# Set 0's routing and placing in tiles of the context, three scatters a step, and the last layer's inverse roots on VectorE

## The chip, the cores and the metric

The kernel runs on one core of one Trainium2 chip. The metric is device time in microseconds (us) of one execution. A profiled execution gives a trace: every instruction of the engines with start and length, the waits between them, the transfers, and the clock granted to TensorE. Engines are named as in the profile: PE (TensorE, matmuls; PEld its weight loads), DVE (VectorE), ACT (ScalarE), POOL (GpSimd), SP (SyncE, which here only issues transfers).

## The reference

A decoder of two layers on x of 32 x 128 tokens by 128 features, everything in float32. Each layer adds three blocks to x, each applied to a layer norm of x without weights:

```python
x = x + L0_attn(ln(x)); x = x + L0_xattn(ln(x), ctx); x = x + L0_ffn(ln(x))
x = x + L1_attn(ln(x)); x = x + L1_xattn(ln(x), ctx); x = x + L1_ffn(ln(x))
```

L1_attn is an attention by random features (16 heads, 32 features each), L1_xattn a softmax attention over ctx (16 heads of 8). The last block, L1_ffn, is a mixture of 16 experts, 4 of them for each token, and one expert for all:

```python
logits = x @ gate_w.T
sel = top_k(logits + expert_bias, 4)
g = softmax(logits[sel])                 # weights of the four
out = swiglu(x, shared) + sum(g[e] * swiglu(x, expert e) for e in sel)
```

## The kernel before, in words

Tokens come in 8 groups (`NG`) of 4 batches (`GB`) of 128 tokens. x and ctx stay in SBUF, as `x0..x7` and `ctx0..ctx7` (`cx[g]` in the code, 128 x 512 each). For the last mixture four sets of 8 batches (`NBR`, two groups) are formed. Set 1 is computed densely: every expert on every token, with weights of zero for those not chosen (`dense_n`). Sets 0, 2 and 3 (`SETS`) are sorted by expert: each token's normalized row is written four times to a table in DRAM (`rows_in`), at places that make the rows of an expert stand together, padded to tiles of 128; then tile after tile is computed with its one expert's weights, written to `rows_out`, and gathered back.

What is done for a sorted set, in `Tables`:

- `route` (line 1997 on): VectorE, with one exponential on ScalarE, makes the four best experts of each token, a one-hot `ones` for each of the four, a `mask`, and the softmax weights `parts`. It is a generator of some 18 pieces; `choose(n, k)` in `mixture` advances it by k pieces, and `routing` runs the first piece.
- `placed` (from line 2034): 18 matmuls on PE count the tokens of each expert (`places`), VectorE turns the counts into a place for each token and choice (`place`), and into the expert that owns each tile (`of`). It has thirteen pieces. The scratch it shares with `route` comes from `two_wide` (two views of 128 x 512) and `square` (128 x 256).
- `way_out` (line 2093): indirect transfers issued by GpSimd, one for each batch and choice, which scatter 128 rows each to `rows_in`: 32 for a set.
- `way_back` (line 2201): the gathers from `rows_out`, again on GpSimd, and `added` (line 2211), which adds them to x on VectorE.

For set 0 the scratch was the tiles `rot` and `rotsin` of the pool `early`, which the first layer-1 attention uses for its rotation until step 29 or 30. For the sets of the last layer it is made in that layer's own pool.

The order of the work is written out by hand. `steps` (line 1188) takes stages as (stage, first step, every, how often). In each step the main stages run their pieces in the order of the list; after each such piece one piece is taken from the stages under `between`, in the order of that list, and what is left of `between` at the end of the step is issued there in one block. Within a region of manual order each engine issues its instructions in exactly this order, so an engine that waits holds back all that is behind it. The second layers (`second_layers`, line 2531) and the last layer (`last_layer`, line 2108) are two such regions; the order between the two on an engine is the scheduler's, as far as the data allow.

In the second layers (their steps run to 45) the stages around the change are: the averages of the cross attention, `xaverage`, one batch a step in steps 13 to 44, each with a 32 x 32 transpose (`by_token`, line 1295), a reciprocal (`rec`, 1297) and three more instructions on VectorE, and after each fourth three instructions on GpSimd (`in_range`, lines 1314 to 1316) which check the reciprocals; `totals` with its `sb` on VectorE (line 2457); `xnorm` in steps 10, 14, ... 38 and `xscaled` one step later, the norm before the cross attention, whose inverse root is GpSimd's (`power`, lines 1097 and 1098) and whose result `xn` (line 1126) PE transposes into `pxn` (line 1135). Set 0's `routing` is in step 25, `choose` in steps 26 and 27 (three pieces each) and 31 and 32 (six each), `placed` in step 33 in one go, `way_out` in steps 35 to 42 with the four scatters of one batch a step, `owned` in step 36.

In the last layer the norms of set 1 are due in step 0, of set 2 in step 1, of set 3 in step 5 (`norm`, line 2118: eight `bn_stats` and `bn_aggr` pairs on VectorE, lines 1115 and 1116, then `power` on GpSimd for each group); `chosen` of set 2 in step 5, its `placed` in step 6, its scatters from step 7; those of set 3 in steps 11, 12 and 13 on. The first tile quads of set 0 are loaded in step 0 (`rows_of`, line 2152: SP loads `rows`, then the weights of four tiles) and transposed by PE in step 1 (`prows`, line 2176). A quad goes through `rows_up` (pg, pu, then the product `sgrows` on VectorE, line 2189) and `rows_down` (`pyrows`). Twelve quads make a set, so set 2's first is needed in step 12.

Of the kernel before, what the change touches and what calls it, by code (L numbers as in the profile page):

```python
# [9 lines left out]
F32 = mybir.dt.float32  # L10
I32 = mybir.dt.int32
AF = mybir.ActivationFunctionType
ALU = mybir.AluOpType
AX = mybir.AxisListType

B, S, D = 32, 128, 128
T = B * S
GB = 4
# [4 lines left out]
E = 16  # L23
# [932 lines left out]
def fast_decoder(ctx: ExitStack, tc: tile.TileContext, ins, spans, out: bass.AP):  # L956
# [3 lines left out]
    nc = tc.nc  # L960

    res = ctx.enter_context(tc.tile_pool(name="res", bufs=1))
    st = ctx.enter_context(tc.tile_pool(name="st", bufs=4))
# [33 lines left out]
    x = [res.tile([128, GB, D], F32, name=f"x{g}") for g in range(NG)]  # L997
    cx = [res.tile([128, GT], F32, name=f"ctx{g}") for g in range(NG)]
# [82 lines left out]
    def rsqrt(dst, src):  # L1081


        n = src.shape[1]
        t = st.tile([128, n], F32, name=f"newton{n}", bufs=2)
        nc.vector.tensor_scalar(t.bitcast(I32), src.bitcast(I32), 1, None, ALU.logical_shift_right)
        nc.vector.tensor_scalar(dst.bitcast(I32), t.bitcast(I32), -1.0, float(0x5F3759DF), ALU.mult, ALU.add)
        for _ in range(3):
            nc.vector.scalar_tensor_tensor(t, dst, -0.5, dst, ALU.mult, ALU.mult)
            nc.vector.tensor_tensor(t, t, src, ALU.mult)  # L1090
            nc.vector.scalar_tensor_tensor(dst, t, 1.5, dst, ALU.add, ALU.mult)
            yield
# [16 lines left out]
    def moments(src):  # L1109

        n = src.shape[1]
        parts = st.tile([128, n, 6], F32, name=f"parts{n}")
        mv = st.tile([128, n, 2], F32, name=f"mv{n}")
        for b in range(n):
            nc.vector.bn_stats(parts[:, b, :], src[:, b, :])
            nc.vector.bn_aggr(mv[:, b, :], parts[:, b, :])  # L1116
            yield
        return mv
# [23 lines left out]
    def norm_factors(g):  # L1142
        mv = yield from moments(x[g])
        return mv, power(mv[:, :, 1], 1e-5, -0.5, "r")

    def layernorm(wk, g):
        return at_once(normed(wk, g, *at_once(norm_factors(g))))

# [543 lines left out]
    NBR = 8  # L1692
# [267 lines left out]
    class Tables:  # L1960


        def __init__(self, early, spare, C):

            self.C = C
            self.xn, self.ones, self.masks, self.parts, self.places, self.of, self.owners = ({} for _ in range(7))
            self.one = by_rows.tile([128, 1], F32, name="one")
            nc.vector.memset(self.one, 1.0)
            self.spare = spare[:, 0 : NBR * D].rearrange("p (g b f) -> p g b f", b=GB, f=D)
            self.wide = lambda: early.tile([128, GB, 2 * D], F32, name="rot", bufs=1).rearrange("p b f -> p (b f)")  # L1970
            self.thin = lambda: early.tile([128, 2, D // 2, 2], F32, name="rotsin", bufs=2).rearrange(
                "p n h d -> p (n h d)"
            )
            self.pool_of_owners = by_rows

        def later(self, wk):

            self.wide = lambda: wk.tile([128, 8 * NBR * E], F32, name="two_wide", bufs=1)
            self.thin = lambda: wk.tile([128, E * E], F32, name="thin", bufs=1)
            self.pool_of_owners = wk  # L1980

        def two_wide(self):

            t = self.wide()
            return (
                t[:, i * 4 * NBR * E : (i + 1) * 4 * NBR * E].rearrange("p (k b e) -> p k b e", k=4, e=E)
                for i in range(2)
            )

        def square(self):  # L1990
            return self.thin().rearrange("p (a b) -> p a b", b=E)
# [98 lines left out]
            self.owners[n] = self.pool_of_owners.tile([1, S], I32, name=f"owner{n}", bufs=1)  # L2090
            nc.vector.tensor_copy(self.owners[n], pt)

        def way_out(self, n, u):
            b, g = u % GB, n * NBR // GB + u // GB
            for k in range(4):
                sent = nc.gpsimd.indirect_dma_start(  # L2096
                    out=rows_in[n],
                    out_offset=bass.IndirectOffsetOnAxis(ap=self.places[n][:, k, u : u + 1], axis=0),
                    in_=self.xn[g][:, b],
                    in_offset=None,  # L2100
                )

                tc.declare_no_dep(sent.ins, group=f"rows{n}", reason="rows of different places")
                tc.add_to_no_dep_group(f"rows{n}", sent.ins)
                nc.gpsimd.nop()
                yield

    def last_layer(tag, W, stages, of_expert, tables):

        wk = phase(tag, mixture_psum)  # L2110
# [5 lines left out]
        of_set = lambda n: range(n * NBR // GB, (n + 1) * NBR // GB)  # L2116

        def norm(g):
            factors[g] = yield from norm_factors(g)

        def scaled(g):
            xn[g] = wk.tile([128, GB, D], F32, name="xr", bufs=6)
# [162 lines left out]
        def each(stage, keys):  # L2285
            return lambda k: stage(*keys[k])

        def several(stage, keys):
            def run(_):
# [5 lines left out]
        dense_n = ({1, 2, 3} - set(SETS)).pop()  # L2295
        n2, n3 = SETS[1:]
        batches = lambda n: [(n, u) for u in range(NBR)]
        once = lambda stage, k, s: (lambda _: stage(k), s, 1, 1)
        steps(
            *((lambda _, i=i: fetched(*i), at_step, 1, 1) for i, at_step in fetches),  # L2300
# [23 lines left out]
                once(chosen, n2, 5),  # L2324
                once(several(norm, of_set(n3)), None, 5),
                once(tables.placed, n2, 6),
                *((each(tables.way_out, batches(n2)[i::2]), 7, 1, 4) for i in range(2)),
                once(several(scaled, of_set(n3)), None, 8),
                once(chosen, n3, 11),
                once(tables.placed, n3, 12),  # L2330
                (each(tables.way_out, batches(n3)), 13, 1, NBR),
                (each(way_back, batches(0)), 21, 1, NBR),
                (each(added, batches(0)), 24, 1, NBR),
                (each(way_back, batches(n2)), 29, 1, NBR),
# [196 lines left out]
    def second_layers(stages, early, late, after, tables):  # L2531

        wk = phase("l1", attention_psum)
        late.append(wk)
        norm, scaled, turn_in, project, turn, features_q, features_k, totals, average, finish = stages
        xnorm, xscaled, xvalues, xkey, xturn, xproject, xweights, xaverage, xfinish = l1_xattn(early, wk)
        rnorm, rscaled, rturn, routing, choose, send, *_ = after
        R = NBR // GB
        first = lambda stage: lambda g: stage(early, g)
        later = lambda stage: lambda g: stage(g + 1)  # L2540
        norm_, scaled_ = later(norm), later(scaled)
        of_four = lambda stage, b, at: (lambda g: stage(g * GB + b), at + b, 4, NG)
        placed = lambda _: tables.placed(0)

        steps(
            (totals, 5, 1, NU),
            (later(turn), 6, 4, NG - 1),
            (finish, 9, 4, NG),
            (xfinish, 17, 4, NG),
            (xvalues, 11, 4, NG),  # L2550
            (features_k, 4, 4, NG),
            (features_q, 3, 4, NG),
            (xturn, 11, 4, NG, xscaled),
            of_four(xweights, 1, 12),
            of_four(xweights, 2, 12),
            (xaverage, 13, 1, NU),
            (later(turn_in), 4, 4, NG - 1),
            (first(rturn), 20, 4, R),
            (xkey, 11, 4, NG),
            of_four(xweights, 3, 12),  # L2560
            (average, 5, 1, NU),
            of_four(xweights, 0, 12),
            (later(project), 5, 4, NG - 1),
            (xproject, 11, 4, NG),
            (first(routing), 25, 1, 1),
            (lambda _: tables.owned(0), 36, 1, 1),
            between=[
                (xscaled, 11, 4, NG),
                (scaled_, 3, 4, NG - 1),
                (norm_, 0, 4, NG - 1),  # L2570
                (xnorm, 10, 4, NG),
                (first(rscaled), 19, 4, R, xturn),
                (first(rnorm), 18, 4, R),
                (lambda _: choose(0, 3), 26, 1, 2),
                (lambda _: choose(0, 6), 31, 1, 2),
                (placed, 33, 1, 1),
                (lambda u: tables.way_out(0, u), 35, 1, NBR),
            ],
            as_written=8,
        )  # L2580
# [41 lines left out]
    with tc.tile_pool(name="l1early", bufs=1, reuse_waits="tile") as early:  # L2622
        late = []
        W1A, W1X, L = (load(name, nc.sync, early) for name in ("w1a", "w1x", "later"))
        with scope():
            stages = []

            def l1_setup(_, k):
                stages.extend(l1_attn(early, late))

            mixture_layer(
                "l0f",
                mixture0,
                ((l1_setup, 10, 1, 1), *((lambda _, k, i=i: stages[i](k), 11 + i, 1, 1) for i in range(5))),
            )
        (W1F, load_w1f), spare = load_wide(nc.sync, "w1f")
        load_w1f()
        C = load("last", nc.sync, by_rows)
        tables = Tables(early, spare, C)
        of_expert = lambda c: (W1F["gud"][:, bass.ts(3 * c + i, 128)] for i in range(3))  # L2640
        mixture1 = mixture("l1f", W1F, lambda lg, _: tables.route(lg, 0), 1, True, of_expert, tables.kept)
        with scope():
            second_layers(stages, early, late, mixture1, tables)
# [37 lines left out]
```

## Time and profile before

| | us |
|---|---|
| three runs | 1398.26, 1410.21, 1411.42; median 1410.21 |
| the profiled execution | 1399.19 |
| its span, first to last instruction | 1397.4 |
| mean granted clock of PE in it | 0.954 of full |
| PE busy | 1251.7 |
| VectorE busy | 860.9 |
| ScalarE busy | 576.9 |
| GpSimd busy | 528.0 |

Times inside the trace are counted from the first instruction. The second layers end at about 1109 us, the last layer fills the rest. "Busy" adds up the lengths of an engine's instructions; where an engine sat idle, the profile names what ended the wait, and the step at fault is the one whose instruction came last. A clock of 0.5 in a stretch means that PE's instructions there take about twice as long.

### The profile page before, as it was taken

How to read it: one execution, taken by the hardware profiler on the slowest of the kernel's cores; microseconds unless marked ns; L12 is line 12 of the kernel's file. 1: busy time of each engine (PE TensorE's matmuls, PEld its weight loads, DVE VectorE, ACT ScalarE, POOL GpSimd, SP SyncE). 2: the span in 40 equal slices, each digit the busy share in tenths (PEclk: the TensorE clock that was granted, in tenths of full speed). 3: DMA queues.
4: the chain of work that ended last, by engine and by line, in shares of the span. 5: the costliest groups of instructions: out<-in, count | busy, mean ns of one | idle time of the engine just before them, and what ended most of it. 6: DMA issues, size and time to landing. Idle time of an engine off the chain costs nothing. (4 is left out here: it accounts for less than half of the span.)

```text
span 1397.4 us, 27515 instructions
## 1 busy us (share of the span) xinstructions
PE 1251.7 (90%) x10753; PEld 842.1 (60%) x10753; DVE 860.9 (62%) x2283; ACT 576.9 (41%) x848; POOL 528.0 (38%) x717
## 2 busy tenths in 40 slices
PE   3689999999999999699999989988987688799997
PEld 2357777777777777444444446655664386577753
DVE  5646767686767675376865535676776346534663
ACT  1354454454554433233232235555553444344432
POOL 5233232434351221132100114344425605576775
PEclk8789999999999999899999999999997879999999
DMA  9601111111212111264164120000000269699943
GB/s 346 186 1 32 32 32 32 32 33 32 51 26 47 36 32 32 64 148 91 32 122 87 36 96 2 2 2 1 2 2 26 70 189 323 201 344 305 330 142 97
DMA packets 89529, 129.07 MB, mean 92 GB/s; under 512 B 9872, under 2 KB 63760, under 8 KB 87984
## 3 DMA queue, kind: packets, MB, share of 16 engines
q1 hardware_dynamic: 76624, 102.59, 26.1%
q0 software_dynamic: 6144, 12.60, 3.1%
q10 hardware_dynamic: 6624, 12.05, 2.3%
q8 instruction: 87, 1.43, 0.5%
q14 instruction: 50, 0.41, 0.1%
HBM read 99.34 MB, written 27.85 MB: 91 GB/s over the span
## 5 line engine op out<-in xcount | busy, mean ns | idle before, releaser
L1280 ACT ACTIVATE e<-scores 128x1024 f32<-128x1024 f32 x128 | 124.0, 1021 | 58.4 <-PE scores L977 58.4
L977 PE MATMUL y<-sg,wide 128*128 128x512 f32 x224 | 117.6, 613 | 7.4 <-DVE sg L2229 2.5
L977 PE MATMUL pg<-hx,wide 128*128 128x512 f32 x224 | 116.0, 599 | 0.0
L977 PE MATMUL pu<-hx,wide 128*128 128x512 f32 x224 | 115.4, 597 | 0.0
L2204 POOL DMA_INDIRECT back<-rows_out,place x96 | 93.4, 973 | 36.4 <-issue 25.2
L1126 POOL TENSOR_SCALAR xn<-x,mv,r 128x128 f32<-128x128 f32 x76 | 63.2, 838 | 91.5 <-PE pxn L1135 82.8
L1295 DVE STREAM_TRANSPOSE by_token<-sums 128x512 f32<-128x512 f32 x64 | 45.6, 713 | 82.1 <-PE sums L977 81.8
L1531 ACT ACTIVATE e<-xscores 128x1024 f32<-128x1024 f32 x64 | 62.0, 1021 | 79.9 <-PE xscores L977 79.9
L1097 POOL TENSOR_SCALAR r<-mv 128x4 f32<-128x4 f32 x48 | 11.5, 240 | 218.7 <-DVE mv L1116 218.3
L1882 ACT ACTIVATE sg<-pg 128x512 f32<-128x512 f32 x72 | 43.0, 597 | 119.4 <-PE pg L977 108.8
L977 PE MATMUL scores<-qb,k 32*128 32x512 f32 x512 | 77.4, 675 | 12.3 <-ACT qb L1466 4.5
L1883 DVE TENSOR_TENSOR sg<-sg,pu 128x512 f32<-128x512 f32 x72 | 49.3, 685 | 61.1 <-PE pu L977 58.1
L977 PE MATMUL sums<-e,v 128*32 128x128 f32 x2048 | 73.8, 285 | 13.6 <-POOL v L1075 10.6
L1097 POOL TENSOR_SCALAR r2x<-mv 128x2 f32<-128x2 f32 x16 | 3.7, 233 | 211.7 <-DVE mv L1116 211.7
L977 PEld LDWEIGHTS sums<-e,v 128*32 128x32 f32 x2048 | 54.8, 113 | 42.2 <-issue 11.3
L2096 POOL DMA_INDIRECT rows_in<-xr,place x64 | 62.5, 976 | 34.6 <-issue 18.0
L1545 DVE COPY v<-pval 128x512 f32<-128x512 f32 x64 | 43.5, 680 | 50.3 <-PE pval L977 50.3
L1579 ACT COPY av<-po 128x512 f32<-128x512 f32 x64 | 37.5, 586 | 89.6 <-PE po L977 89.5
L977 PEld LDWEIGHTS pu<-hx,wide 128*128 128x128 f32 x224 | 42.6, 191 | 52.5 <-issue 50.1
L977 PE MATMUL po<-e,v 128*64 128x128 f32 x1024 | 65.3, 279 | 8.6 <-DVE v L1545 8.6
L977 PE MATMUL po<-av,wide 128*128 128x256 f32 x256 | 63.3, 403 | 8.6 <-DVE av L1599 8.6
L977 PEld LDWEIGHTS y<-sg,wide 128*128 128x128 f32 x224 | 35.9, 189 | 58.0 <-DVE sg L1885 36.7
(301 smaller groups left out, 2906.7 us busy)
## 6 DMA issues: line engine op xcount, KB each, us to landing
row_weights<-in_w1f_dram SPq DMA_DIRECT2D x144, 192.0 KB, 4.3
factor<-factors SPq DMA_DIRECT2D x64, 256.0 KB, 5.1
share<-combined SPq DMA_DIRECT2D x32, 512.0 KB, 10.3
rows_in<-in_few SPq DMA_DIRECT2D x36, 256.0 KB, 4.1
rows<-rows_in SPq DMA_DIRECT2D x36, 256.0 KB, 5.3
rows_out<-yrows ACTq DMA_DIRECT2D x36, 256.0 KB, 4.0
share<-combined SPq DMA_DIRECT2D x8, 1024.0 KB, 9.3
wide<-in_w1f_dram SPq DMA_DIRECT2D x1, 3272.0 KB
```

Source lines behind the costliest of these rows:

```text
L977: last[0] = nc.tensor.matmul(*args, **kw)
L1097: nc.gpsimd.tensor_scalar(t, src, add, None, ALU.add)
L1126: eng.tensor_scalar(n[:, b, :], x[g][:, b, :], mv[:, b, 0:1], r[:, b : b + 1], ALU.subtract, ALU.mult)
L1280: nc.scalar.activation(e[-1], ps[:, bass.ts(n, 2)].rearrange("p c i s -> p (c i) s"), AF.Exp, scale=scale)
L1295: nc.vector.transpose(tt.rearrange("p i t r -> p (i t r)"), po.rearrange("p i s -> p (i s)"))
L1531: nc.scalar.activation(e[-1], ps[:, n].rearrange("p r c s -> p (r c) s"), AF.Exp, scale=scale)
L1545: nc.vector.tensor_copy(v[:, bass.ts(n, XC), :], pv)
L1579: nc.scalar.copy(avs[w][n][:, :, bass.ts(b, S)], po)
L1882: nc.scalar.activation(sg, pg, AF.Silu)
L1883: nc.vector.tensor_tensor(sg, sg, pu, ALU.mult)
L2096: sent = nc.gpsimd.indirect_dma_start(out=rows_in[n], out_offset=bass.IndirectOffsetOnAxis(ap=self.places[n][:, k, u : u + 1], axis=0), in ...
L2204: nc.gpsimd.indirect_dma_start(out=outs[n, u][:, k], out_offset=None, in_=rows_out[n], in_offset=bass.IndirectOffsetOnAxis(ap=places[n][:, ...
```

## The change

Set 0's scratch is now three context tiles: `cx[0]` and `cx[1]` for the two wide views, the first 256 columns of `cx[2]` for the square. The context of a group is last read by `xvalues` and `xkey` of that group, in steps 11, 15 and 19 for these three. `two_wide` takes two tiles instead of two halves of one, in the last layer too.

With that scratch the pieces are laid out anew: `choose` advances by three pieces in each of the steps 26 to 31; the thirteen pieces of `placed` go by five in steps 32, 33 and 34 (`some_of`); `way_out` takes a list of (batch, choice) and issues three scatters in each of the steps 35 to 45, the last two of the 32 in step 45. In the last layer `way_out` gets the same four of a batch as before.

The last layer's `norm` takes its inverse roots from `norm_factors_by_vector`: one addition, and then `rsqrt`, which is the bit trick and three Newton steps, eleven instructions on VectorE, all on 128 x 4.

```diff
+    def norm_factors_by_vector(g):
+        mv = yield from moments(x[g])
+        ve = st.tile([128, GB], F32, name="ve", bufs=2)
+        nc.vector.tensor_scalar(ve, mv[:, :, 1], 1e-5, None, ALU.add)
+        r = st.tile([128, GB], F32, name="rv", bufs=2)
+        yield from rsqrt(r, ve)
+        return mv, r
...
-            self.wide = lambda: early.tile([128, GB, 2 * D], F32, name="rot", bufs=1).rearrange("p b f -> p (b f)")
-            self.thin = lambda: early.tile([128, 2, D // 2, 2], F32, name="rotsin", bufs=2).rearrange(
-                "p n h d -> p (n h d)"
-            )
+            self.wide = lambda: [cx[i] for i in (0, 1)]
+            self.thin = lambda: cx[2][:, 0 : E * E]
...
-            self.wide = lambda: wk.tile([128, 8 * NBR * E], F32, name="two_wide", bufs=1)
+            self.wide = lambda: [wk.tile([128, 4 * NBR * E], F32, name=f"wide{i}", bufs=1) for i in range(2)]
...
-        def way_out(self, n, u):
-            b, g = u % GB, n * NBR // GB + u // GB
-            for k in range(4):
+        def way_out(self, n, some):
+            for u, k in some:
+                b, g = u % GB, n * NBR // GB + u // GB
...
         def norm(g):
-            factors[g] = yield from norm_factors(g)
+            factors[g] = yield from norm_factors_by_vector(g)
...
-        placed = lambda _: tables.placed(0)
+        placing = []
+        to_send = [(u, k) for u in range(NBR) for k in range(4)]
+
+        def some_of(placing, n):
+
+            if not placing:
+                choose(0)
+                placing.append(tables.placed(0))
+            for _ in range(n):
+                if next(placing[0], "end") == "end":
+                    return
+                yield
...
-                (lambda _: choose(0, 3), 26, 1, 2),
-                (lambda _: choose(0, 6), 31, 1, 2),
-                (placed, 33, 1, 1),
-                (lambda u: tables.way_out(0, u), 35, 1, NBR),
+                (lambda _: choose(0, 3), 26, 1, 6),
+                (lambda n: some_of(placing, 5), 32, 1, 3),
+                (lambda i: tables.way_out(0, to_send[3 * i : 3 * i + 3]), 35, 1, 11),
```

The helper that the new norms call, which the kernel had for another use:

```python
    def rsqrt(dst, src):
        n = src.shape[1]
        t = st.tile([128, n], F32, name=f"newton{n}", bufs=2)
        nc.vector.tensor_scalar(t.bitcast(I32), src.bitcast(I32), 1, None, ALU.logical_shift_right)
        nc.vector.tensor_scalar(dst.bitcast(I32), t.bitcast(I32), -1.0, float(0x5F3759DF), ALU.mult, ALU.add)
        for _ in range(3):
            nc.vector.scalar_tensor_tensor(t, dst, -0.5, dst, ALU.mult, ALU.mult)
            nc.vector.tensor_tensor(t, t, src, ALU.mult)
            nc.vector.scalar_tensor_tensor(dst, t, 1.5, dst, ALU.add, ALU.mult)
            yield
```

More of the change, by code (lines that the diff above doesn't have):

```diff
@@ L1960, in fast_decoder, with __init__ @@
     class Tables:
-        def __init__(self, early, spare, C):
+        def __init__(self, spare, C):
             self.C = C
@@ L1982, in two_wide @@
         def two_wide(self):
[L1984 to L1988, printed above, removed]
+            return (t.rearrange("p (k b e) -> p k b e", k=4, e=E) for t in self.wide())
         def square(self):
@@ L2297, in last_layer @@
         batches = lambda n: [(n, u) for u in range(NBR)]
+        to_send = lambda n: [(n, [(u, k) for k in range(4)]) for u in range(NBR)]
         once = lambda stage, k, s: (lambda _: stage(k), s, 1, 1)
@@ L2326, in last_layer @@
                 once(tables.placed, n2, 6),
-                *((each(tables.way_out, batches(n2)[i::2]), 7, 1, 4) for i in range(2)),
+                *((each(tables.way_out, to_send(n2)[i::2]), 7, 1, 4) for i in range(2)),
                 once(several(scaled, of_set(n3)), None, 8),
@@ L2330, in last_layer @@
                 once(tables.placed, n3, 12),
-                (each(tables.way_out, batches(n3)), 13, 1, NBR),
+                (each(tables.way_out, to_send(n3)), 13, 1, NBR),
                 (each(way_back, batches(0)), 21, 1, NBR),
@@ L2638, in fast_decoder @@
         C = load("last", nc.sync, by_rows)
-        tables = Tables(early, spare, C)
+        tables = Tables(spare, C)
         of_expert = lambda c: (W1F["gud"][:, bass.ts(3 * c + i, 128)] for i in range(3))
```

## The prediction, on record before the run

> **What bounds the kernel now.** The page first: TensorE is busy nine tenths of the span, so time is lost only where TensorE waits, and where its clock drops after a wait.
>
> ```profile
> PE 1251.7 (90%) x10753; PEld 842.1 (60%) x10753; DVE 860.9 (62%) x2283; ACT 576.9 (41%) x848; POOL 528.0 (38%) x717
> ```
>
> Next the table by stretches around the change: the second layers' last steps (to about 1109 us) and the last layer. Columns: stretch, length, busy time (count) of PE, PE weight loads, VectorE, ScalarE, GpSimd, then the granted clock, DMA share, GB/s.
>
> ```profile
> 1030.00:1040.00 10.00, 9.03 (x111) 7.19 (x111) 6.02 (x15) 4.64 (x5) 1.86 (x6) 1.00 0.01 2
> 1040.00:1050.00 10.00, 5.89 (x72) 4.38 (x71) 9.31 (x32) 2.10 (x3) 0.00 (x0) 0.81 0.00 0
> 1050.00:1060.00 10.00, 8.17 (x54) 4.40 (x52) 4.58 (x14) 1.27 (x2) 6.01 (x7) 0.51 0.05 15
> ...
> 1110.00:1120.00 10.00, 4.82 (x19) 4.14 (x20) 0.85 (x4) 2.46 (x3) 1.49 (x4) 0.55 0.65 180
> ```
>
> VectorE is full (9.31 of 10) where PE is at its worst, then PE runs ten microseconds at half clock. The timeline of PE names the waits (start, length, instruction, in brackets the idle time before it and its releaser).
>
> ```profile
> 1046.77 1.08 PE L977 MATMUL fsums<-qphi,sb 128*32 128x128 f32 x16 [4.11 <-DVE sb L2457]
> 1080.45 1.47 PE L1135 MATMUL pxn<-in_few,xn 128*128 128x128 f32 x4 [5.59 <-DVE xn L1126]
> 1114.45 1.09 PE L2176 MATMUL prows<-in_few,rows 128*128 128x128 f32 x4 [5.42 <-DMA rows<-rows_in]
> 1212.41 1.08 PE L2176 MATMUL prows<-in_few,rows 128*128 128x128 f32 x4 [6.76 <-DMA rows<-rows_in]
> ```
>
> The first is the placing of set 0 drained at one step's end, ahead of `sb` on VectorE's queue. The third and fourth are sets 0 and 2 waiting for the last scatter. GpSimd's timeline shows how the scatters end and what their start waits for:
>
> ```profile
> 1108.08 0.96 POOL L2096 DMA_INDIRECT rows_in<-wide,place  x1 [0.30 <-DVE rec L1297]
> 1109.34 0.96 POOL L2096 DMA_INDIRECT rows_in<-wide,place  x1 [0.30 <-issue]
> 1110.38 0.56 POOL L1314 TENSOR_SCALAR in_range<-rec 128x64 f32<-128x64 f32 x1
> ...
> 1167.54 1.09 POOL L2096 DMA_INDIRECT rows_in<-xr,place  x1 [5.91 <-DVE expert_ends L2082]
> ```
>
> Set 2's 32 scatters start as soon as VectorE has placed and run without a gap to 1208.5. The chain that ended last runs back through them into VectorE's work of 1149 to 1167, set 3's eight statistics (1156.93 to 1160.0) included. From 1230 on PE and GpSimd are both full, so a shift of 1212 is a shift of the end.
>
> **The change part by part** (negative is a gain).
>
> *Placing over steps 32 to 34.* The thirteen pieces were all due in step 33; now five come in step 32, five in 33, three in 34, one per stage of PE's work. From step 32's `by_token` (1029.60) to the last statistic before the cross-attention's next group (1051.06) VectorE needs 21.5 us, 3.8 of them waits for PE (0.75, 1.57, 0.68, 0.77). The last three pieces (1044.91 to 1046.30, 1.4 us) move behind the statistics; of the waits I take half as filled, 1.9: -3.3. What is late next is that group's `xn`, after GpSimd's two-step root (0.23 and 1.04 us). With the long stall gone, 1053.04 to 1060.3 should run at full clock: pxn, sums, pk, scores then take 0.66, 1.08, 1.13, 1.14 and a 0.4 wait, 4.4 instead of 7.3: -2.9. Together -6.2. Ends: -8.7 (the whole 4.11, and 4.6 for fsums, pS, pval, sums, pk, scores, which took 1.08, 1.97, 2.02, 1.94, 2.08, 1.71 us here and 0.62, 1.10, 1.11, 1.08, 1.13, 1.14 at full clock), and -1.4. I take the middle, nearer the better end, since VectorE is the bound there.
>
> [...] The row shows 13 us at half. [...]
>
> *Routing over steps 26 to 31.* `ones`, mask, product, reductions (0.89, 0.3, 0.77, 0.68, 0.4, 0.4, 0.2 us) leave steps 31 and 32 for 28 to 31: some 3 us of VectorE work into 999 to 1020, where it is busy 7.0 and 7.7 of 10 us and PE is nearly full. Hidden by those gaps: +0.5; all of it would be +3.1 if the rotation's inputs slip. The tiles ctx0 to ctx2 were last read in step 19; nothing waits for them. The exponential moves two steps on ScalarE, which has a gap of 3.36 us at 1017 to 1020: nothing. The last layer's wide tile cut in two holds the same bytes and costs nothing. The 18 `places` matmuls (2.1 us) only change step.
>
> *Three scatters a step.* In the code step 44 first runs the last average with its three `in_range` instructions on GpSimd, and only then step 44's three scatters and step 45's two. Before, all 32 stood ahead of that check. GpSimd's queue is in order, so five scatters now wait for `rec` of the last batch (done at 1107.82 before). Then: check 1.36 (1110.38 to 1111.74), gap 0.17, four pitches of 1.264 and one of 0.96: the last scatter ends 7.6 us after `rec`, before 2.5 (1110.30). Behind it stand SyncE's first `rows` load and the four weight loads queued after that, and PE's prows. +5.1. Ends: +1.3 if only step 45's two stood behind the check, +6.5 if GpSimd is also late from earlier steps (steps of 3.3 us, 3.8 us of scatters).
>
> *Roots by VectorE.* Each group drops GpSimd's 0.23 and 1.04 us and adds twelve VectorE instructions on 128x4, each dependent on the last. No row has one in such a chain: bounds are 0.15 (L2085, 128x1, 153 ns) and 0.21 (start to start of L2061, 128x16, and its successor). I take 0.19, nearer the upper since the chain is dependent: 2.3 a group, 4.56 a set (3.6 to 5.0).
> Set 2 (step 1): the instructions follow 1125.5 and push `sgrows` of quad 1 (1128.99); 0.87 of waiting for PE and 0.28 for GpSimd's root cover part: +3.4.
> Set 3 (step 5): they stand at 1160.0 between its statistics and set 2's placing, on a queue without gaps to 1167: +4.56, straight into the scatters' start.
> At 0.15 and 0.21 the two come to +6.0 and +8.9.
> Set 1 (step 0): nothing in the last layer's region orders it behind the second layers, and its eight statistics run already at 1072 to 1076 in step 38, ahead of the 5.59 us stall. Another 4.56 us may go there or into the gaps of 1081 to 1106 (2.47, 2.09, 3.55, 1.82, 1.44). I take +1.0 because of those gaps; ends 0 and +4.6. The 2.5 us that GpSimd loses at 1091 to 1094 had nobody waiting: nothing.
>
> [...]
>
> *Clock in the last layer.* PE would wait 3.4 us more at 1129.7, and after the 3.94 us wait at 1133 the table shows half clock for eleven. pyrows, pg and pu of the next quad (2.9 us) may double: +1.0, ends 0 and +2.9.
>
> Sum: -6.2 + 0.5 + 5.1 + 3.4 + 4.6 + 1.0 + 1.0 = **+9.4 us**. Against the profiled execution (1399.19, span 1397.4) that is 1408.6. The three runs are 1398.26, 1410.21 and 1411.42, so the four executions form two groups; on their mean, 1404.8, the change gives **1414**.
>
> **The rivals.**
> *A: not slower; VectorE's roots are covered.* Place: 1121 to 1167. If PE, at half clock after the longer wait for the scatters, is later than VectorE throughout, set 2's 3.4 us vanish, and set 3's go if the products of the quads are what is waited for. For it: PE was at half clock at 1114 to 1128 and 1138 to 1149. Against it: VectorE has no gap from 1149.5 to 1167. Price: -8.0 and no clock term, +0.4, 1405. It decides once more than 8 of the 9.4 us are hidden.
> *B: slower by over 1%; set 1's roots land at the stall.* All 4.6 us ahead of `xn` at 1080.05, a PE wait of 9 to 10 us, and half clock for as long as after 1046 (4.6 us lost): +9.4 + 3.6 + 4.6 = +17.6, 1422. For it: the statistics already lie there. Against: the gaps after 1081.
> *C: the placing is still a stall.* The pieces of steps 33 and 34 stand ahead of `sb` as before and the clock stays down: -1.4 instead of -6.2, +14.2, 1419. For it: step 33 holds 7 us of VectorE work against 5.8 of PE's. Against: one piece per stage leaves no block.
>
> **How the numbers follow.** Forecast 0.53, A 0.17, B 0.16, C 0.14. For the forecast alone I take +3 to +14 (from the ends of the terms), 1408 to 1419 on the mean base, 1402 to 1425 with the two groups. With A below (1399 in the lower group) and half of B above, 1400 to 1427 leaves out two in ten. About 1% is what a measurement of this kernel can tell from no change (14 us, as wide as the spread of its runs). Slower by more: most of B, a third of C, a little of the forecast, 0.22. Faster by more: a small part of A, if the placing also reaches its end of -8.7 and the base is the lower group, 0.05. Within: 0.73.
>
> **What would show it.** The 4.11 us wait before fsums is gone and the clock is 1.0 at 1050 to 1060 (placing). Five rows_in scatters follow the last in_range, and the wait before the first prows is near 10.5 us (scatters). Twelve 128x4 VectorE instructions a group at 0.15 to 0.21 us; set 2's scatters start some 14 us later after the last `rec` than the 59.7 now (scatters and roots). It is wrong if the scatters end within 3 us of `rec`, if PE's wait at 1080 doubles (B), or if set 2's scatters start no later after `rec` (A).

## The result and the profile after

The changed kernel takes 1415.75 us (median of 20 runs, 1407.85 to 1428.51), the kernel before 1407.17 us (20 runs, 1398.26 to 1416.72). The ratio is 1.0081 with a 95% interval of 1.0056 to 1.0106: some 11 us (8 to 15) slower; the medians differ by 8.6. Ratios leave out runs more than 1.5% above the fastest of their kernel, which matters for e1 below (4 of 12 runs; the ratio of the means is 1.004 with them) and for e13 (3 of 12; 0.999 with them). The profiled execution of the changed kernel took 1414.33 us, its span is 1412.6 and the mean clock 0.951.

A single span says little about a part, since profiles differ by ten microseconds and more ahead of most of the changed work: PE's last `qkv` of step 29 starts between 1007 and 1021 us in the fourteen profiles of this study, and e5 (1007) and e3 (1020), which ran on one chip, are alike up to there. I therefore count from that instruction. From there to the end the kernel before takes 387.9 us, the changed one 404.6. That is +16.7, more than the ratio's +11.4; it is one execution of each, and 1.6 of it is a clock that another execution of the same kernel does not show (last section).

The page after the change: VectorE has 72 instructions more (six groups of twelve), GpSimd 12 fewer.

```profile
PE 1254.9 (89%) x10753; PEld 842.6 (60%) x10753; DVE 870.9 (62%) x2355; ACT 577.8 (41%) x848; POOL 520.5 (37%) x705
```

The table by stretches, with the same columns as before:

```profile
1030.00:1040.00 10.00, 9.21 (x167) 6.98 (x162) 7.97 (x19) 5.93 (x6) 1.87 (x6) 1.00 0.01 2
1040.00:1050.00 10.00, 5.89 (x80) 4.26 (x79) 9.45 (x35) 2.01 (x3) 1.31 (x2) 0.83 0.00 0
1050.00:1060.00 10.00, 9.12 (x122) 5.48 (x124) 4.52 (x12) 5.89 (x8) 5.99 (x7) 0.83 0.10 30
...
1110.00:1120.00 10.00, 3.07 (x10) 2.14 (x10) 0.00 (x0) 1.87 (x2) 1.48 (x2) 0.50 0.50 149
```

The clock at 1050 to 1060 is 0.83 instead of 0.51, with 122 matmuls instead of 54 in the same ten microseconds: the placing's gain. At 1110 to 1120 PE did ten instructions instead of nineteen: the scatters' loss. PE's timeline shows where the waits went:

```profile
1042.43 0.64 PE L977 MATMUL fsums<-qphi,sb 128*32 128x128 f32 x16
...
1048.80 0.66 PE L1135 MATMUL pxn<-in_few,xn 128*128 128x128 f32 x2 [3.75 <-DVE xn L1126]
...
1076.55 1.47 PE L1135 MATMUL pxn<-in_few,xn 128*128 128x128 f32 x4 [6.91 <-DVE xn L1126]
...
1115.86 1.09 PE L2178 MATMUL prows<-in_few,rows 128*128 128x128 f32 x4 [10.57 <-DMA rows<-rows_in]
...
1135.57 2.04 PE L977 MATMUL pyrows<-row_weights,sgrows 128*128 128x128 f32 x8 [5.23 <-DVE sgrows L2191]
...
1224.49 1.08 PE L2178 MATMUL prows<-in_few,rows 128*128 128x128 f32 x4 [5.46 <-DMA rows<-rows_in]
```

`fsums` waits no more (4.11 before), `pxn` behind it waits 3.75 (1.47), the stall of step 38 is 6.91 (5.59), the first `prows` waits 10.57 (5.42), and `pyrows` of quad 1 waits 5.23 for `sgrows` (0.41 before). GpSimd's timeline gives the cause of the fourth, and the start of set 2's scatters, 75.6 us after the last `rec` (59.7 before):

```profile
1104.24 0.45 POOL L1322 TENSOR_SCALAR in_range<-rec 128x64 f32<-128x64 f32 x1 [0.96 <-DVE rec L1305]
...
1105.65 1.08 POOL L2098 DMA_INDIRECT rows_in<-wide,place  x1 [0.16 <-issue]
...
1110.82 0.96 POOL L2098 DMA_INDIRECT rows_in<-wide,place  x1 [0.30 <-issue]
...
1179.71 0.95 POOL L2098 DMA_INDIRECT rows_in<-xr,place  x1 [67.93 <-DVE expert_ends L2084]
```

VectorE's timeline in step 38 shows set 1's roots ahead of the cross-attention's `xn`, for which PE waits 6.91 us. The first group's chain runs from 1069.01 to 1071.35:

```profile
1069.01 0.17 DVE L1149 TENSOR_SCALAR ve<-mv 128x4 f32<-128x4 f32 x1
1069.21 0.17 DVE L1086 TENSOR_SCALAR newton<-ve 128x4 int32<-128x4 int32 x1
...
1071.19 0.16 DVE L1091 SCALAR_TENSOR_TENSOR rv<-newton,rv 128x4 f32<-128x4 f32 x1
...
1076.15 1.34 DVE L1126 TENSOR_SCALAR xn<-x,mv,r 128x128 f32<-128x128 f32 x4 [0.92 <-POOL r L1098]
```

### The profile page after: what moved, and what is told of

Read it like the earlier page. It is cut to its first block, busy times and chain, and to the rows that moved or that the text cites. A ratio compares the mean times of both kernels' runs of the same rounds, so it can differ in the third digit from the quotient of the medians.

```text
span 1412.6 us, 27577 instructions
## 1 busy us (share of the span) xinstructions
PE 1254.9 (89%) x10753; PEld 842.6 (60%) x10753; DVE 870.9 (62%) x2355; ACT 577.8 (41%) x848; POOL 520.5 (37%) x705
## 5 line engine op out<-in xcount | busy, mean ns | idle before, releaser
L1288 ACT ACTIVATE e<-scores 128x1024 f32<-128x1024 f32 x128 | 124.0, 1021 | 57.2 <-PE scores L977 57.2
L977 PE MATMUL y<-sg,wide 128*128 128x512 f32 x224 | 118.4, 617 | 12.5 <-DVE sg L2231 7.5
L1539 ACT ACTIVATE e<-xscores 128x1024 f32<-128x1024 f32 x64 | 62.0, 1021 | 79.9 <-PE xscores L977 79.9
L2191 DVE TENSOR_TENSOR sgrows<-sgrows,pu 128x512 f32<-128x512 f32 x36 | 24.7, 687 | 76.1 <-PE pu L977 61.4
```

What stands on the lines that cost most here:

```text
L977: last[0] = nc.tensor.matmul(*args, **kw)
L1288: nc.scalar.activation(e[-1], ps[:, bass.ts(n, 2)].rearrange("p c i s -> p (c i) s"), AF.Exp, scale=scale)
L1539: nc.scalar.activation(e[-1], ps[:, n].rearrange("p r c s -> p (r c) s"), AF.Exp, scale=scale)
L2191: nc.vector.tensor_tensor(sg, sg, pu, ALU.mult)
```

## The experiments

The theory is the prediction's sum: placing gains, while the scatters behind the last check and VectorE's roots cost more. The main rivals are A (the roots are covered) and B (set 1's roots land at the stall of step 38).

The runs came in three groups, each on one chip with runs of the kernel before beside it. In the first that kernel took 1408 us (1407 above, which I count with this group); in the second 1536 and in the third 1543, on two other chips. Ratios are therefore to the kernel before of the same group.

This table counts from one event to the next in each profile (us). "Block" is the stretch from step 30's `pxn` to the next `pxn`, "stall" from there to the `pxn` of step 38. Then come the end of set 0's last scatter, the first `prows`, and set 2's first scatter, all after the last `rec`.

| kernel | group | ratio, 95% interval | block | stall | last scatter | prows | set 2 |
|---|---|---|---|---|---|---|---|
| before | 1 | 1 | 32.78 | 27.41 | 2.48 | 6.63 | 59.72 |
| changed | 1 | 1.0081 (1.0056 to 1.0106) | 28.37 | 27.75 | 7.71 | 11.79 | 75.64 |
| e1 roots by GpSimd | 1 | 1.0017 (0.9976 to 1.0058) | 28.37 | 26.28 | 7.72 | 11.90 | 68.72 |
| e2 before + roots by VectorE | 1 | 1.0077 (1.0041 to 1.0113) | 32.77 | 28.34 | 0.17 | 4.08 | 69.58 |
| e3 four scatters a step | 1 | 1.0035 (1.0001 to 1.0069) | 28.38 | 27.64 | -0.08 | 3.97 | 68.66 |
| e5 all ahead of the check | 1 | 1.0077 (1.0043 to 1.0110) | 28.38 | 27.67 | 5.51 | 9.42 | 75.08 |
| e4 set 3's norm later | 2 | 1.0099 (1.0066 to 1.0133) | 28.37 | 31.01 | 7.70 | 11.84 | 70.93 |
| e6 placing in one block | 2 | 1.0115 (1.0062 to 1.0167) | 32.66 | 30.32 | 7.72 | 11.94 | 76.72 |
| e8 spread alone | 2 | 0.9963 (0.9929 to 0.9996) | 28.38 | 32.79 | -10.08 | 2.06 | 53.11 |
| e9 spread, set 3's norm later | 2 | 0.9990 (0.9952 to 1.0028) | 28.38 | 33.51 | -9.32 | 2.37 | 57.08 |
| e10 changed, again | 3 | 1.0109 (1.0073 to 1.0145) | 28.37 | 30.60 | 7.70 | 11.78 | 76.90 |
| e11 spread alone, again | 3 | 0.9956 (0.9925 to 0.9986) | 28.37 | 33.12 | -10.36 | 2.38 | 51.49 |
| e12 as e4, again | 3 | 1.0060 (1.0030 to 1.0091) | 28.38 | 31.29 | 7.73 | 11.87 | 70.64 |
| e13 as e9, again | 3 | 0.9959 (0.9921 to 0.9996) | 28.36 | 34.24 | -10.70 | 2.07 | 59.02 |

**e1: the roots back on GpSimd.**

```diff
-            factors[g] = yield from norm_factors_by_vector(g)
+            factors[g] = yield from norm_factors(g)
```

> The changed kernel with the last layer's inverse roots given back to GpSimd, all else as changed. Theory: VectorE's roots cost the changed kernel 3.4 to 3.7 us ahead of set 2's sgrows, 4.8 us ahead of set 2's placing (the pos copy stood 12.2 us later after the change, 7.4 already before set 3's norm) and some 1.3 us at the stall of step 38; together 9 us less. GpSimd gets 2.5 us of set 1's roots back among its 17 last scatters of set 0, so that their end can come 2.5 us later: 6 to 9 us below the changed kernel, a ratio to the kernel before of 1.001 to 1.004, and set 2's scatters start 63 to 68 us after the last rec (75.6 changed, 59.7 before). Rival (roots covered by PE's own waits, prediction's A): ratio stays at 1.008 and set 2's scatters start 75 us after rec.

Measured: ratio 1.0017 against 1.0081, some 9 us less by these ratios; set 2's scatters start 68.7 us after the last `rec`. From PE's timeline, and then from GpSimd's:

```profile
1075.68 1.47 PE L1135 MATMUL pxn<-in_few,xn 128*128 128x128 f32 x4 [5.61 <-DVE xn L1126]
...
1114.97 1.08 PE L2178 MATMUL prows<-in_few,rows 128*128 128x128 f32 x4 [10.69 <-DMA rows<-rows_in]
```

```profile
1171.79 1.09 POOL L2098 DMA_INDIRECT rows_in<-xr,place  x1 [5.91 <-DVE expert_ends L2084]
```

The stall of step 38 is back at 5.61, so the 1.3 us there were set 1's roots. The scatters do not end 2.5 us later, as I had thought possible: GpSimd did set 1's roots between 1079 and 1087, ahead of the last check but one, where it had time. Rival A falls here: by the trace the scatters start 6.9 us earlier without VectorE's roots.

**e2: the kernel before, with the roots by VectorE.** The edit is the reverse of e1's, on the kernel before.

> The kernel before with the last layer's inverse roots by VectorE, and nothing else changed. Theory: plus 8 us at set 2's scatters (3.5 and 4.8), less up to 2.5 us because GpSimd no longer does set 1's roots between set 0's scatters; plus 1 us if set 1's chain lands at the stall of step 38: +5 to +9 us, ratio 1.004 to 1.0065. Set 2's scatters start 66 to 69 us after the last rec instead of 59.7. Rival (covered): ratio 1.000, scatters at 60 us after rec.

Measured: 1.0077, nearly the whole loss of the change, and 69.6 us after `rec`; both just over the range I gave. From PE's timeline:

```profile
1052.88 1.08 PE L977 MATMUL fsums<-qphi,sb 128*32 128x128 f32 x16 [4.11 <-DVE sb L2465]
...
1138.74 2.04 PE L977 MATMUL pyrows<-row_weights,sgrows 128*128 128x128 f32 x8 [4.00 <-DVE sgrows L2197]
```

GpSimd does end its scatters 2.3 us earlier (0.17 after `rec`, not 2.48). But from the first `prows` to set 2's first scatter it takes 65.50 us against 53.09: +12.4, of which set 3's chain is 4.8 and 7.6 lie before it. What I left out is the second line: the 4.00 us wait that set 2's roots put in front of `pyrows` halves PE's clock, and `pyrows` takes 2.04 us instead of 1.16.

**e3: four scatters a step.**

```diff
-    (lambda i: tables.way_out(0, to_send[3 * i : 3 * i + 3]), 35, 1, 11),
+    (lambda i: tables.way_out(0, to_send[4 * i : 4 * i + 4]), 35, 1, 8),
```

> The changed kernel with four scatters a step over steps 35 to 42 in place of three over 35 to 45. Theory: GpSimd issues three more of them before the check of the last batch but one and none behind the last check, so the last scatter ends 1 to 2.5 us after the last rec (7.7 changed), the wait before the first prows falls from 10.6 to between 4 and 5.5 us, and the kernel takes 5 to 6.5 us less than the changed one: ratio 1.003 to 1.0045. Rival (the bubble is hidden by VectorE's later queue, which is what sets 1121 to 1167): ratio stays at 1.008, prows come earlier and sgrows do not.

Measured: 1.0035, some 6 us less than the changed kernel, with intervals that overlap between 1.0056 and 1.0069. GpSimd's timeline:

```profile
1114.46 0.96 POOL L2098 DMA_INDIRECT rows_in<-wide,place  x1 [0.30 <-issue]
1115.67 0.45 POOL L1322 TENSOR_SCALAR in_range<-rec 128x64 f32<-128x64 f32 x1 [0.25 <-DVE rec L1305]
```

The last scatter now stands ahead of the check and ends 0.1 us before `rec` does, earlier than in the kernel before (2.5 after it) and than I expected. The wait before the first `prows` is 2.76 us, where I wrote 4 to 5.5, and `prows` comes 7.8 us earlier after `rec` than in the changed kernel.

**e5: all 32 ahead of the last check, with the same first fifteen.**

```diff
-    (lambda i: tables.way_out(0, to_send[3 * i : 3 * i + 3]), 35, 1, 11),
+    (
+        lambda i: tables.way_out(0, to_send[3 * i + max(0, i - 5) : 3 * i + 3 + (0, 1, 2, 3, 5)[max(0, i - 4)]]),
+        35,
+        1,
+        9,
+    ),
```

> The changed kernel with the scatters of steps 40 on packed closer (4, 4, 4, 5 in steps 40 to 43), so that the same 15 come in steps 35 to 39 as in the changed kernel but all 32 stand ahead of the last batch's check. It parts two readings of the late scatters. If the place behind the check is the cause (the prediction's sum), the last scatter ends 2.5 us after rec, as before, and the whole 5.1 us come back. If GpSimd's queue is the cause (17 scatters of 1.264 us left after the check of the last batch but one, which ends at 1088.1, whatever their place), they end at 1109.6, 2.2 us earlier than in the changed kernel, the wait before prows is 8.3 us, and only the check and its wait (2.2 us) come back: ratio 1.006 to 1.007.

GpSimd's timeline, and the first `prows` from PE's:

```profile
1107.56 0.96 POOL L2098 DMA_INDIRECT rows_in<-wide,place  x1 [0.30 <-issue]
1108.60 0.43 POOL L1322 TENSOR_SCALAR in_range<-rec 128x64 f32<-128x64 f32 x1
```

```profile
1112.43 1.09 PE L2178 MATMUL prows<-in_few,rows 128*128 128x128 f32 x4 [8.20 <-DMA rows<-rows_in]
```

The scatters are all ahead of the check, and still end 5.51 us after `rec`, with no gap between them; the wait is 8.20 us where I wrote 8.3. So only 2.2 of the 7.7 us come from the place behind the check (1.3 us of it, and the wait for `rec`). The rest is GpSimd's queue: at three a step too few scatters are done before the last check but one, for which GpSimd waits, and seventeen of 1.264 us each are left behind it. The time (1.0077) cannot tell 2 us from none.

**e6: the placing in one step again.**

```diff
-    (lambda n: some_of(placing, 5), 32, 1, 3),
+    (lambda n: some_of(placing, 20), 33, 1, 1),
```

> The changed kernel with set 0's placing put back into one step (33); routing, scatters and roots as changed. Theory: the wait before fsums of 4.1 us and the half clock after it come back, the wait before pxn falls from 3.75 to about 1.5 us; from step 30's pxn to the next cross-attention's pxn 32.8 us instead of 28.4, so 4 to 5 us more than the changed kernel, ratio 1.011 to 1.012. Rival (one late thing only takes the place of another): ratio unchanged.

PE's timeline:

```profile
1059.97 1.08 PE L977 MATMUL fsums<-qphi,sb 128*32 128x128 f32 x16 [4.11 <-DVE sb L2460]
...
1066.24 0.66 PE L1135 MATMUL pxn<-in_few,xn 128*128 128x128 f32 x2 [1.47 <-DVE xn L1126]
```

The stall of 4.11 us is back to the hundredth, and the block takes 32.66 us, as in the kernel before, against 28.4 in all eleven profiles with the placing spread. By the trace the spread gains 4.3 us in the block. From there to step 38's `pxn` the one block takes 0.7 us less (30.32 against 31.01 in e4, on the same chip), so that 3.6 are left. By the time it stays undecided: 1.0115 with an interval of a per cent, and the changed kernel did not run in that group.

**e4 and e12: set 3's norm two steps later.**

```diff
-                once(several(norm, of_set(n3)), None, 5),
                 once(tables.placed, n2, 6),
+                once(several(norm, of_set(n3)), None, 7),
```

> The changed kernel with set 3's norm (eight statistics, 3.2 us, and two chains of roots, 4.8 us) moved from step 5 to step 7 of the last layer, so that set 2's placing stands ahead of it on VectorE. Theory (VectorE's queue from 1150 to 1170 is what set 2's scatters wait for): they start 6 to 8 us earlier, 68 to 70 us after the last rec instead of 75.6, and the kernel takes 4 to 8 us less than the changed one, ratio 1.0025 to 1.005; less if SyncE's and PE's wait for y's sg (5.5 us before y) grows instead. Rival (those scatters do not hold the end): they start earlier and the ratio stays at 1.008.

> The changed kernel with set 3's norm moved from step 5 to step 7, beside the changed kernel. Theory: set 2's scatters start 5 to 7 us earlier after the last rec than the 75.6 of the changed kernel (70.9 in the second group), and the time falls by as much: ratio to the kernel before 1.002 to 1.005. Rival (what the scatters win is lost again at the wait for set 2's last one or for set 3's first): they start earlier, ratio 1.007 or more.

Measured: set 2's scatters start 70.6 us after `rec`, against 76.9 of the changed kernel in the same group (e10), 6.3 us earlier. The ratio is 1.0060 beside 1.0109, with intervals that overlap between 1.0073 and 1.0091. The first run of the same kernel gave 1.0099, which misses what I expected of it, and it had no changed kernel in its group. So the earlier start is shown, and a gain in time is not.

**e8 and e11: the spread alone.** Roots as in e1 and scatters as in e3, both edits on the changed kernel.

> The first half of the change alone: routing and placing spread over their steps as changed, four scatters a step, roots by GpSimd. Theory: from step 30's pxn to the next pxn 28.4 us instead of 32.8; the last scatter ends 0 to 3 us after the last rec; set 2's scatters start 58 to 62 us after it, as before (59.7): 4 to 6 us below the kernel before, ratio 0.996 to 0.997. Rival (the gain is given back further on, by GpSimd's scatters now closer to the last rec): ratio 1.000.

> The spread of routing and placing alone (four scatters a step, roots by GpSimd) beside the changed kernel. Theory: 0.996 to 0.998 of the kernel before (0.9963 in the second group), 384 us from step 29's qkv to the end; the last scatter ends 0 to 3 us after the last rec. Rival (the gain of the placing, 4.4 us, is given back where set 0's rows are waited for): 1.000.

Measured: 0.9963 and 0.9956, faster than the kernel before by some 0.4% in both groups, with both intervals below 1 (the first by 0.0004). This is the version that beats both kernels; the first chip did not run it. From `rec` to set 2's first scatter it takes 53.1 and 51.5 us, less than I expected, since on these two chips the last scatter ends 10 us before `rec`. GpSimd's timeline of e8:

```profile
1112.90 0.96 POOL L2098 DMA_INDIRECT rows_in<-wide,place  x1 [0.30 <-issue]
1124.11 0.45 POOL L1322 TENSOR_SCALAR in_range<-rec 128x64 f32<-128x64 f32 x1 [10.25 <-DVE rec L1305]
```

On these chips PE itself is late here (see the end). GpSimd's queue is empty early (in e10 too, 12.28 us ahead of the check), and only scatters that stand behind the check are late: the place of five scatters, worth 2.2 us on the first chip, costs 9.4 here (`prows` 11.78 after `rec` in e10, 2.38 in e11).

**e9 and e13: the spread alone, with set 3's norm later.** The edits of e8 and of e4 together.

> The spread alone, with set 3's norm also moved behind set 2's placing (roots by GpSimd). Theory: set 2's scatters start another 3 us earlier after the last rec (55 to 58 us), and the kernel takes 6 to 9 us less than the one before, ratio 0.9935 to 0.996. Rival: what set 3's norm leaves is filled by PE's products and the ratio is that of the spread alone.

> The spread alone with set 3's norm behind set 2's placing, beside the changed kernel. Theory: like the spread alone less up to 3 us, 0.993 to 0.997 of the kernel before. Rival: set 2's scatters start earlier and set 3's norm is then late for its own scaling and scatters: 0.997 to 1.000.

Measured: 0.9990 and 0.9959, no better than the spread alone; the theory fell. Half of it held once: VectorE has set 2's places ready 3.0 us earlier after `rec` in e9 than in e8, but 0.5 us later in e13 than in e11. Set 2's scatters start later in both (57.1 and 59.0 against 53.1 and 51.5). VectorE's timeline of e13, last instruction of the placing, and then GpSimd's:

```profile
1175.20 0.15 DVE L2087 TENSOR_SCALAR of<-of 128x1 f32<-128x1 f32 x1
```

```profile
1178.38 0.23 POOL L1097 TENSOR_SCALAR r<-mv 128x4 f32<-128x4 f32 x1 [41.82 <-DVE mv L1116]
...
1182.09 1.09 POOL L2098 DMA_INDIRECT rows_in<-xr,place  x1 [0.18 <-issue]
```

The places are ready at 1175.3, but set 3's two roots stand ahead of the scatters in GpSimd's queue and wait for their statistics until 1178.38. With roots by VectorE (e4) nothing stands there. Issuing that norm behind the first scatters was not tried.

**e10: the changed kernel again.**

> The changed kernel unchanged, for a second profile and as the partner of the three kernels beside it: every kernel of the second group of runs took 9% longer than in the first, the one before included, and none of that group was the changed one. Expected on a chip like the first: ratio 1.006 to 1.011; from step 29's qkv to the end 400 to 407 us (404.6 in the first profile, 387.9 before), with the half clock of step 30 (1.6 us) either there or not.

Measured: 1.0109; the block is 28.37 again, the last scatter ends 7.70 us after `rec` again. The half clock of step 30 is not there. From step 29 to the end it is 543.8 us on this chip, where I had named the first chip's figures only.

## Why the prediction was right

The forecast was 1414, the median is 1415.75; the sum was +9.4, the ratio says +11.4 (8 to 15), the medians 8.6. That the forecast lies within 2 us is in part luck: the base it starts from, 1404.8, was 2.4 us below the median of the kernel before over 20 runs, and by the profiles the parts add up to more than the sum. Five of the seven terms have the right size, two of them (placing and scatters) by a reason that is right only in part; the routing term cannot be read; the clock is mis-sized, and what lies behind set 2's scatters was left out. The measured side is the difference of the two first profiles, counted from step 29.

| step of the prediction | predicted | measured | where it is seen |
|---|---|---|---|
| placing over steps 32 to 34 | -6.2 | -5.5 | `pxn` 4.4 earlier (block); from there to step 38 without set 1's roots (e1) -1.13 |
| routing over steps 26 to 31 | +0.5 | 0 or +1.6 | step 29's `qkv` to step 30's `pxn`: 10.78 before, 12.42 after, 10.79 in e1 and e10 |
| set 1's roots | +1.0 | +1.5 | stall 27.75 against 26.28 in e1 |
| three scatters a step | +5.1 | +5.2 | `prows` 11.79 after `rec`, 6.63 before |
| set 2's roots | +3.4 | +3.1 | `pyrows` to `sgrows` of quad 1: 4.66 before, 7.76 after |
| set 3's roots | +4.6 | +4.8 | `places` to the `pos` copy: 5.71 before, 10.49 after |
| clock in the last layer | +1.0 | +2.9 | rest of `prows` to set 2's scatters: 1.2 before quad 0's `pyrows` (0.64 of it a wait for weights), 1.6 behind the new wait |
| behind set 2's scatters | 0 | +3.0 | set 2's first scatter to the end: 229.89 before, 232.84 after |

With +0.15 before the last `rec` these make the +16.7.

*Placing.* The total holds, but its two halves are both off and make up for each other. The `pxn` behind the placing comes 4.4 us earlier, where I had 3.3. The four steps from it to `scores`, for which I wrote 4.4 us instead of 7.3 at full clock, take 6.3 (6.1 in e1): 1.0 to 1.1 gained, not 2.9. The "late next" is `xn` as I said, but PE waits 3.75 us for it, so the half clock is not gone but shorter, from PE's start at 1048.8 to about 1053.5, with one wait of 0.36 in it.

*Routing.* The +1.6 is no cost of the moved pieces: `scores` and `sums` of step 30 ran at half clock in one execution and at full clock in another of the same kernel (last section). What the pieces themselves cost does not show: where the clock stayed up, the stretch is as long as before.

*Scatters.* The size was right by luck, since half of the reason was not. I put all of it down to five scatters behind the last check. By e5 the place is 2.2 us; the rest is the queue, which the prediction had only at its upper end ("if GpSimd is also late from earlier steps").

*Roots.* The row prices held: twelve instructions every 0.198 us, 4.75 us for the 24 of a set (0.19 taken). Each is busy for 0.16 to 0.17 us here; but this chain, whose links wait for each other, pays the pitch, 0.198.

*Clock.* This is the mis-sized term, +2.9 for +1.0. That it equals the upper end I gave is luck, for I had only the new wait in mind, which is worth 1.6. Ahead of it, the wait for `rows` is twice as long and PE's half clock lasts longer behind it (to 9.3 us after `prows`, 6.8 before), and `pg` waits 0.64 us for its weights, which land late too; then the 5.23 us wait before quad 1's `pyrows` brings it once more (`pyrows` and `pg` 2.04 and 1.73 us, 1.16 and 1.06 before). In e1 that second wait is gone, yet set 2's scatters come only 6.9 us earlier, where the two chains would be 7.9: the half clock behind `prows` lasted longer there (to 17.3 us after `prows`; `logits` 3.54 us, 1.93 in the changed kernel).

*What the sum left out.* Behind set 2's scatters I wrote that a shift of 1212 is a shift of the end. `y` after set 2's `prows` waits 2.01 us for `sg` (0.33 before), the clock is halved once more behind that wait (`pg` and `pu` 1.91 and 1.73 us, 1.02 each before), and the end comes 3.0 us later than by the shift.

*The rivals.* A is wrong by e1 and e2: by their ratios the roots cost 9 to 11 us of time. B is right in its place and mostly wrong in its price: fourteen of set 1's 24 root instructions stand ahead of `xn`, and the stall grew by 1.3 us, not by 4. C is wrong: the wait for `sb` is gone.

What stays open: why the two profiles differ by 16.7 us behind step 29 when the ratio says 11.4 and the medians 8.6. The clock of step 30, 1.6 us, depends on the execution, and other half clocks may; profiles of the first chip differ by up to 12.5 us ahead of that point.

## What to carry to other kernels

GpSimd worked through its queue in order here, and what it still had to do behind each wait (seventeen scatters of 1.264 us behind the last check but one, five of them behind the last) set the price, not only which instruction stood last: count what is left at the last two waits, before you say what a reordering costs. The roots, moved off an idle engine onto one that feeds the end, cost their whole chain, at the pitch between dependent instructions (0.198 us) and not their busy time (0.16 to 0.17), and once more in PE's clock where they opened a new wait (1.6 us behind the wait of 5.23). One profile does not size that clock, since the same waits cost more or less of it from one execution to the next (1.6 us in step 30). When a change has several parts, run each alone: here one part gained 0.4% (on two other chips) and two others hid it.

## What the runs showed of the hardware

**The same waits, another clock.** PE's timeline of the changed kernel's first profile and then of its second (e10), at the same instructions:

```profile
1011.68 0.77 PE L2414 MATMUL prot<-in_few,rot 128*128 128x128 f32 x5 [0.36 <-POOL rot L2405]
1012.37 2.00 PE L977 MATMUL scores<-qb,k 32*128 32x512 f32 x8
```

```profile
1021.85 0.77 PE L2414 MATMUL prot<-in_few,rot 128*128 128x128 f32 x5 [0.36 <-POOL rot L2405]
1022.54 1.14 PE L977 MATMUL scores<-qb,k 32*128 32x512 f32 x8
```

The waits ahead of `prot` are the same in both (0.22, 0.58, 0.36 us), and `scores` takes 2.00 us in one and 1.14 in the other. The stretch from step 29's `qkv` to step 30's `pxn` takes 12.4 us in six of the fourteen profiles and 10.8 in eight.

The traces show what sorts them. All 662 changes of the granted clock in the fourteen profiles lie, within 0.03 us (0.01 in the kernel before and in the changed one), on a grid with a pitch of 3.413 us, and where the grid lies differs from one execution to the next. In the six slower profiles a line of it falls 0.5 to 0.8 us after the start of the `prot` row above, and the clock is halved there for one pitch (0.50 from 1012.52 to 1015.93 in the first profile). In the eight others the line falls 1.3 to 2.3 us after it, and the clock stays (2.3 us, and 1.00, in the kernel before). So the same short waits cost clock in some executions and not in others, which may be a part of the scatter between runs.

Apart from the one that the end cuts off, each half clock in the profiles of the kernel before and of the changed one lasts whole pitches, one to six of them. Around set 0's placing it lasts four in the kernel before (1046.14 to 1059.80), two in the changed kernel (1046.65 to 1053.48) and one in e1 (1050.34 to 1053.75), though the last two have the same wait of 3.75 us. In the kernel before PE was busy for 0.82, 0.59 and 0.88 of the first three pitches, and the clock stayed at half (0.50); it came back (1.00) after the fourth, which PE filled (3.41 us of 3.41). The prediction's 13 us at half clock are nearly four such pitches, with the waits of 1.47 and 0.36 us inside them.

**Chips that stop elsewhere.** On the chips of the second and third group every kernel took 9 to 10% longer. PE's timeline of e10 shows stops inside one group of 32 `sums`, and the longest wait in the last layer; then VectorE's shows what `pyrows` waited for:

```profile
1106.86 0.56 PE L977 MATMUL sums<-e,v 128*32 128x128 f32 x7
1108.42 0.41 PE L977 MATMUL sums<-e,v 128*32 128x128 f32 x4 [1.00 <-issue]
1109.88 0.42 PE L977 MATMUL sums<-e,v 128*32 128x128 f32 x4 [1.04 <-issue]
...
1249.90 2.07 PE L977 MATMUL pyrows<-row_weights,sgrows 128*128 128x128 f32 x8 [31.20 <-DVE sgrows L2191]
```

```profile
1249.16 0.69 DVE L2191 TENSOR_TENSOR sgrows<-sgrows,pu 128x512 f32<-128x512 f32 x1 [33.79 <-remote]
```

PE stops for a microsecond every few matmuls though it waits for nothing that the profile names. From step 38's `pxn` to the last `rec` that makes 39.0 us instead of the 27.5 of the first chip. But most of the loss lies further on: from set 2's first scatter to the end it takes 358.2 us in e10 and 232.8 in the first profile of the same kernel. There PE has eleven waits of over 3 us, 99 us together; in the longest, of 31.20 us, VectorE stands still as well, and what releases it the profile calls only remote. The cause was not tried. It changes what a part is worth, as the five scatters show.
